# Masked ids mapped by GpSimd ahead of each chunk's gathers, instead of by VectorE once per block

## The chip, the cores and the metric

One core of one Trainium2 chip runs the kernel. The metric is the device time of one execution in microseconds (us); a value is the median of some runs. The program uses the core's five engines: TensorE (PE in the profile, PEld for its weight loads), VectorE (DVE), ScalarE (ACT), GpSimd (POOL) and SyncE (SP). Times are compared within the same rounds on the same chip. Where costs per chunk from different jobs stand side by side, each is taken against the kernel before in its own rounds.

## The reference

A recommendation model: for each of 16384 users, 69 item ids are looked up in a table of 96-wide float32 rows, weighted by a small attention network against a label item, pooled and passed through three dense layers. What matters here is the lookup and its mask:

```python
u = emb[batch_user]                        # 16384 x 69 rows of 96 floats
eff = (batch_user < ITEM_NUM)[..., None]   # ITEM_NUM = 100000; id 100000 is masked
pre = jnp.where(eff, u * att, 0.0)         # a masked token adds nothing
```

The kernels get the mask for nothing by appending a zero row (index 100001) to the table and turning id 100000 into 100001: `row = id + (id >= 100000)`. If the gathered row is zero, so is `u * att`.

## The kernel before

The users are handled in 32 blocks of 512. A block has 69 chunks of 512 tokens (64 main, 5 tail), and a chunk is fetched by four gathers of 128 rows each. Two chunks are a pair; there are 1104 pairs and 2208 chunks. The builder accepts one index per partition for an indirect gather, so one gather fetches at most 128 rows.

```python
def map_ids(n, ids):                       # once per block, 21 steps ahead of its use
    rows = ipool.tile([P, NT], I32, tag="rows", name=f"rows{n}")      # 128 x 276
    nc.vector.scalar_tensor_tensor(rows, ids[:, 0:NT], float(ITEM_NUM), ids[:, 0:NT], ALU.is_ge, ALU.add)
    return rows
...
def fetch(i):                              # one pair of chunks
    u = upool.tile([P, 8, E], F32, tag="u", name=f"u{i}")             # 14 buffers
    ...
    for j in range(2):
        n, k = chunk(2 * i + j)
        ...
        for t in range(4):
            gather(u[:, 4 * j + t, :], rows[n][:, 4 * k + t : 4 * k + t + 1])   # GpSimd
            nc.tensor.transpose(ptr[:, t * P : (t + 1) * P], u[:, 4 * j + t, :], ident)
        ...                                # products on VectorE and ScalarE
```

The attention products follow two steps after the gathers, the pooling products eight; the latter free the `u` buffer.

## Time and profile before

| | before |
|---|---|
| timed, median of 3 (lowest to highest) | 11363.58 us (11353.27 to 11365.34) |
| the one profiled execution | 13499.4 us |
| GpSimd / TensorE busy in it | 63% / 75% |
| a gather: reported time; start to start | 0.951 us; 1.251 us |
| mean granted TensorE clock | 0.658 |

The profiled execution is 2136 us longer than the timed ones; the prediction has to decide what to do about that. In it TensorE hardly ever waits for a gather. This is the row of its waits (who waited <- for what: us in all, times, longest):

```profile
PE ptr L308 <- DMA u<-in_emb,rows: 13.2, 11, 2.0
```

### The profile page before, as it was taken

How to read it: one execution, taken by the hardware profiler on the slowest of the kernel's cores; microseconds unless marked ns; L12 is line 12 of the kernel's file. 1: busy time of each engine (PE TensorE's matmuls, PEld its weight loads, DVE VectorE, ACT ScalarE, POOL GpSimd, SP SyncE). 2: the span in 40 equal slices, each digit the busy share in tenths (PEclk: the TensorE clock that was granted, in tenths of full speed). 3: DMA queues.
4: the chain of work that ended last, by engine and by line, in shares of the span. 5: the costliest groups of instructions: out<-in, count | busy, mean ns of one | idle time of the engine just before them, and what ended most of it. 6: DMA issues, size and time to landing. Idle time of an engine off the chain costs nothing.

```text
span 13499.4 us, 108113 instructions
## 1 busy us (share of the span) xinstructions
PE 10109.4 (75%) x41348; PEld 5068.4 (38%) x41348; DVE 3172.4 (24%) x5424; ACT 3740.6 (28%) x6086; POOL 8525.6 (63%) x8966
## 2 busy tenths in 40 slices
PE   4777777778777776777777777777778777787778
PEld 2333333334333333333333333333333333343334
DVE  2222222222222222222222222222222222222222
ACT  1222222223222222222222222222222222232222
POOL 6666666666666666666666666666666666666664
PEclk5666666666666677666666666766666666666657
DMA  1111111111111111111111111111111111111111
GB/s 37 34 34 35 33 34 33 34 35 34 34 34 34 34 34 33 33 34 34 33 34 34 34 34 35 34 33 33 33 35 34 34 33 34 35 34 33 34 32 22
DMA packets 295008, 453.59 MB, mean 34 GB/s; under 512 B 145952, under 2 KB 151104, under 8 KB 294496
## 3 DMA queue, kind: packets, MB, share of 16 engines
q0 software_dynamic: 286720, 440.98, 15.5%
q8 instruction: 331, 5.42, 0.2%
q1 hardware_dynamic: 6142, 4.77, 0.1%
q14 instruction: 181, 1.48, 0.0%
q10 hardware_dynamic: 1634, 0.94, 0.0%
HBM read 446.04 MB, written 0.07 MB: 33 GB/s over the span
## 4 chain that ended last, share of the span: by engine, by line
PE 62%; another core or an unknown queue 15%; issue 12%; ACT 5%; DVE 5%; POOL 1%; DMA 0%; DVEq 0%; POOLq 0%; ACTq 0%
PE ph L326 22%; PE acc L376 15%; PE ptr L308 9%; PE p L406 5%; PE prow L337 4%; PE ph L278 4%; DVE y L330 3%; ACT y L329 2%; PE patt L353 2%; ACT y L328 1%; PE pa L346 1%; DVE quT L311 1%; ACT uT L319 1%; POOL u L227 1%
## 5 line engine op out<-in xcount | busy, mean ns | idle before, releaser
L227 POOL DMA_INDIRECT u<-in_emb,rows x8832 | 8401.6, 951 | 4802.4 <-issue 2351.7
L376 PEld LDWEIGHTS acc<-rw,u 128*96 128x96 f32 x16384 | 2185.5, 230 | 2828.8 <-issue 2828.2
L278 PE MATMUL ph<-zrow 1*128 1x512 bf16 x1104 | 532.2, 482 | 2654.8 <-DVE y L330 1760.5
L319 ACT COPY uT<-ptr 96x512 f32<-96x512 f32 x2208 | 1285.2, 582 | 3713.4 <-DVE quT L311 2616.7
L376 PE MATMUL acc<-rw,u 128*96 128x20 f32 x16384 | 2298.9, 292 | 1.8 <-DVE rw L359 1.3
L308 PEld LDWEIGHTS ptr<-ident,u 128*96 128x96 f32 x8832 | 1312.6, 167 | 1912.8 <-issue 1547.8
L308 PE MATMUL ptr<-ident,u 128*96 128x128 f32 x8832 | 1785.7, 362 | 326.1 <-issue 247.9
L326 PE MATMUL ph<-uT,A 96*64 96x512 f32 x4416 | 1954.0, 955 | 27.4 <-issue 26.7
L326 PE MATMUL ph<-quT,w 96*64 96x512 f32 x4416 | 1915.7, 909 | 54.5 <-issue 53.2
L328 ACT ACTIVATE y<-ph 128x512 f32<-128x512 f32 x1104 | 659.4, 597 | 4602.9 <-remote 2107.1
L330 DVE TENSOR_TENSOR y<-ph,y 128x512 f32<-128x512 f32 x1104 | 763.7, 692 | 4689.6 <-ACT y L329 2396.5
L311 DVE TENSOR_TENSOR quT<-ptr,qT 96x512 f32<-96x512 f32 x2048 | 1340.0, 680 | 1866.9 <-remote 887.1
L385 DVE COPY pooled<-acc 96x160 f32<-96x160 f32 x1008 | 430.6, 427 | 2811.6 <-remote 1020.7
L326 PEld LDWEIGHTS ph<-quT,w 96*64 96x64 f32 x4416 | 491.4, 202 | 1279.1 <-issue 1277.6
L329 ACT ACTIVATE y<-y,a1c,na1c 128x512 f32<-128x512 f32 x1104 | 897.4, 813 | 37.2
L281 ACT COPY ph<-cT 128x512 f32<-128x512 f32 x1008 | 591.4, 587 | 281.5 <-remote 75.0
L406 PE MATMUL p<-pooled,wf 96*100 96x512 f32 x1280 | 620.0, 625 | 6.3 <-issue 4.8
L337 PE MATMUL prow<-y,v 128*32 128x512 f32 x2208 | 546.6, 932 | 79.7 <-issue 41.3
L326 PEld LDWEIGHTS ph<-uT,A 96*64 96x64 f32 x4416 | 307.0, 183 | 766.4 <-issue 696.0
L339 ACT COPY row<-prow 128x512 f32<-128x512 f32 x276 | 161.4, 585 | 864.0 <-remote 345.4
L353 PE MATMUL patt<-ident,row 128*128 128x128 f32 x1104 | 267.9, 386 | 113.4 <-DVE pre L347 88.1
L406 PEld LDWEIGHTS p<-pooled,wf 96*100 96x100 f32 x1280 | 219.7, 181 | 270.1 <-issue 267.3
(71 smaller groups left out, 2535.6 us busy)
## 6 DMA issues: line engine op xcount, KB each, us to landing
u<-in_emb,rows POOLq DMA_INDIRECT x8832
ids<-in_idx SPq DMA_DIRECT2D x32, 140.0 KB
q<-in_emb,ids POOLq DMA_INDIRECT x128
wf<-in_Wf ACTq DMA_DIRECT2D x1, 825.0 KB
out<-res SPq DMA_DIRECT2D x32, 2.0 KB
w<-in_W SPq DMA_DIRECT2D x1, 96.0 KB
wf<-in_Wf ACTq DMA_DIRECT2D x1, 62.5 KB
a1c<-in_a SPq DMA_DIRECT2D x2, 0.2 KB
```

The costliest lines, as they stand in the source:

```text
L227: nc.gpsimd.indirect_dma_start(out=dst, out_offset=None, in_=emb, in_offset=bass.IndirectOffsetOnAxis(ap=index, axis=0),)
L278: nc.tensor.matmul(ph, zrow[:, 0:P], zrow, start=True, stop=False)
L308: nc.tensor.transpose(ptr[:, t * P : (t + 1) * P], u[:, 4 * j + t, :], ident)
L311: nc.vector.tensor_tensor(quT[:, j, :].rearrange("e (s f) -> e s f", f=FM), ptr.rearrange("e (s f) -> e s f", f=FM), by_field(q[:, k * NS ...
L319: nc.scalar.copy(uT[:, j, :], ptr)
L326: nc.tensor.matmul(ph[j * H1 : (j + 1) * H1, :], w, x[:, j, :], start=False, stop=last)
L328: nc.scalar.activation(y, ph, AF.Sigmoid, scale=S_DICE)
L329: nc.scalar.activation(y, y, AF.Identity, bias=a1c, scale=na1c)
L330: nc.vector.tensor_mul(y, ph, y)
L337: nc.tensor.matmul(pr[32 * k : 32 * (k + 1), :], v2, y, start=True, stop=True)
L376: nc.tensor.matmul(pa[:, j, 2 * t : 2 * t + 2, :].rearrange("e n g -> e (n g)"), u[:, 4 * j + t, :], rw[:, i % 4, j, t, :], start=True, st ...
L406: nc.tensor.matmul(p1, w[:, h * DH : (h + 1) * DH], x, start=(k == 0), stop=(k == KTOP - 1))
```

## The change

The intent is to take the mapping off VectorE and put it on the engine that uses its result, in small pieces that need only small buffers. GpSimd has no fused compare-and-add that compiles (the same `scalar_tensor_tensor` on GpSimd did not compile), so it takes two instructions on a 128x4 tile.

```diff
-    def map_ids(n, ids):
-        rows = ipool.tile([P, NT], I32, tag="rows", name=f"rows{n}")
-        nc.vector.scalar_tensor_tensor(rows, ids[:, 0:NT], float(ITEM_NUM), ids[:, 0:NT], ALU.is_ge, ALU.add)
+    def map_ids(name, ids, k):
+        rows = ipool.tile([P, 4], I32, tag="rows", bufs=8, name=name)
+        i = ids[:, 4 * k : 4 * k + 4]
+        nc.gpsimd.tensor_scalar(rows, i, float(ITEM_NUM), None, ALU.is_ge)
+        nc.gpsimd.tensor_tensor(rows, rows, i, ALU.add)
         return rows
...
+            rows = map_ids(f"rows{i}_{j}", ids[n], k)
             for t in range(4):
-                gather(u[:, 4 * j + t, :], rows[n][:, 4 * k + t : 4 * k + t + 1])
+                gather(u[:, 4 * j + t, :], rows[:, t : t + 1])
...
-            at(first - 21, lambda n=n: rows.__setitem__(n, map_ids(n, ids[n])))
```

More of the change, by code (lines that the diff above doesn't have):

```diff
@@ L103, in load_ids @@
         return ids
-    def map_ids(n, ids):
-        rows = ipool.tile([P, NT], I32, tag="rows", name=f"rows{n}")
-        nc.vector.scalar_tensor_tensor(rows, ids[:, 0:NT], float(ITEM_NUM), ids[:, 0:NT], ALU.is_ge, ALU.add)
-        return rows
-    ids, rows = {0: load_ids(0)}, {}
-    rows[0] = map_ids(0, ids[0])
+    def map_ids(name, ids, k):
[3 more added lines that the diff above has]
+        nc.gpsimd.tensor_tensor(rows, rows, i, ALU.add)
+        return rows
+    ids = {0: load_ids(0)}
     ident = const.tile([P, P], F32, name="ident")
```

## The prediction

> **What bounds the kernel now.** I read the page first, then GpSimd's instructions in order of time, then who waited for whom, then the table of stretches, and last the trace's events.
>
> The page's head and the two rows that matter:
>
> ```profile
> span 13499.4 us, 108113 instructions
> PE 10109.4 (75%) x41348; PEld 5068.4 (38%) x41348; DVE 3172.4 (24%) x5424; ACT 3740.6 (28%) x6086; POOL 8525.6 (63%) x8966
> PE 62%; another core or an unknown queue 15%; issue 12%; ACT 5%; DVE 5%; POOL 1%; DMA 0%; DVEq 0%; POOLq 0%; ACTq 0%
> L227 POOL DMA_INDIRECT u<-in_emb,rows x8832 | 8401.6, 951 | 4802.4 <-issue 2351.7 <-PE acc L376 860.1 <-remote 755.3
> ```
>
> Taken at its word this says TensorE-bound: PE is busiest and is 62% of the chain. But this one profiled execution took 13499 us and the three timed ones 11363.58 us in the median, 2136 us less, so the profile shows the kernel with something in it that the timed runs do not have. Which engine sets 11364 us has to be worked out.
>
> GpSimd in order of time, where nothing holds it up:
>
> ```profile
> 13354.67 0.95 POOL L227 DMA_INDIRECT u<-in_emb,rows  x1 [0.30 <-issue]
> 13355.92 0.94 POOL L227 DMA_INDIRECT u<-in_emb,rows  x1 [0.30 <-issue]
> ...
> 13368.43 0.94 POOL L227 DMA_INDIRECT u<-in_emb,rows  x1 [0.30 <-issue]
> ```
>
> These are 12 gathers; 13368.43 - 13354.67 = 13.76 us over 11 steps is 1.251 us from start to start: 0.95 us of work and 0.30 us in which GpSimd waits for nothing that the profile shows, but cannot start the next. So the 63% of the page understates GpSimd: while it gathers it is full. There are 8832 + 128 = 8960 gathers (the 128 fetch the label rows), and 8960 x 1.251 = 11209 us. The first starts at 3.3 us; the last starts at 13368.4 us and the span ends at 13499.4 us, so some 130 us of draining follow. 3 + 11209 + 130 = 11342 us, 22 us (0.2%) below the timed median. The timed kernel therefore looks bound by the issue of gathers, from end to end.
>
> Why the profiled execution is longer:
>
> ```profile
> POOL u L227 <- issue: 2351.7, 7703, 0.6
> POOL u L227 <- PE acc L376: 860.1, 160, 39.9
> POOL u L227 <- remote: 755.3, 239, 6.0
> POOL u L227 <- PE ptr L308: 447.0, 177, 4.7
> ```
>
> The first row is the 0.30 us between gathers (2351.7 / 7703 = 0.305). The others, with the smaller rows of this view, are 4802.4 - 2351.7 = 2451 us in which GpSimd waited, nearly all for a `u` buffer that TensorE had not yet freed. In the same trace I added up the stretches over 3 us without any TensorE record: 313 of them, 2210 us. An example is 3007 to 3028 us, in which DVE and ACT also stand still and GpSimd goes on until its buffers are full:
>
> ```profile
> 3020.86 0.94 POOL L227 DMA_INDIRECT u<-in_emb,rows  x1 [0.30 <-issue]
> 3027.59 0.95 POOL L227 DMA_INDIRECT u<-in_emb,rows  x1 [5.79 <-remote]
> ```
>
> The chain books such stretches as "another core or an unknown queue" (15% of 13499 us = 2025 us). 2210 us of TensorE silence, 2025 us of unknown chain, and an excess of 2136 us over the timed runs are about the same amount; I read the stalls as belonging to the profiled execution. Without them, a pair of chunks costs TensorE 9.1 us (median over the 492 pairs whose TensorE gaps all stay below 1 us) and GpSimd 8 x 1.251 = 10.0 us. GpSimd is slower by a tenth.
>
> **What the Trainium skill says.** GPSIMD Engine Reference, section 2.1 Instruction dispatch: an instruction is broadcast and dispatched in software on eight cores and counts as complete when all eight have read and their writes have landed in SBUF; consecutive GpSimd instructions are no barrier between cores, so dependent ones need a semaphore wait. The trace agrees in the one place that has such a pair, the building of the identity:
>
> ```profile
> 0.74 0.20 POOL masks.py:197 MEMSET ident<- 128x128 f32 x1 [0.29 <-POOLq L547]
> 1.02 0.29 POOL masks.py:199 TENSOR_SCALAR_AFFINE_SELECT ident<-ident 128x128 f32<-128x128 f32 x1
> ```
>
> The second waits for the first's semaphore in the built program of the kernel before, and starts 0.08 us after its end. Perfetto Trace Analysis, section GPSIMD Engine Instruction, says to time GpSimd from start to start and not by reported durations; that is why I use 1.251 and not 0.951 us. SBUF — State Buffer, section Who interferes with whom: a VectorE instruction with two SBUF inputs blocks GpSimd instructions that read SBUF. The trace before has no steady GpSimd reads, so it can't say; the candidates are the `rw` products (276 of 826 ns) and the last layers' products, together under 3% of the time. GPSIMD Engine Reference, section 4.1 Engine selection, sends elementwise work to VectorE; the present mapping there costs 32 x 432 ns = 14 us on an engine 24% busy.
>
> **The change part by part.**
> Removed: the 32 VectorE instructions, 14 us off the bound. Worth nothing. The first block's mapping ran before the first gathers and delays none (first gather 3.3 us, first `u` gather 8.6 us).
> Added: per chunk of four gathers two GpSimd instructions on 128x4 int32, 2208 chunks, 4416 instructions. They stand in GpSimd's own stream immediately before the gathers that read them, so nothing hides them: GpSimd is strictly in order and full. For one chunk, from the end of its predecessor's last gather:
> - gap to the compare: 0.30 us, taken as that between gathers;
> - compare: 0.12 us (a guess between the one-column memsets, 0.10 to 0.12 us, and the 128-column select, 0.29 us);
> - gap to the add, with its wait for the compare: 0.07 us, from the identity pair;
> - add, two inputs: 0.14 us, likewise;
> - wait of the first gather for the add, up to its start: 0.20 us, the median from a TensorE event to the start of the gather that it released (424 cases, 0.26 us at most).
> Sum 0.83 us, in place of the 0.30 us gap that was there: 0.53 us more per chunk. 2208 x 0.53 = 1170 us, all on the path: 11364 + 1170 = 12534 us, which I round to 12530.
> Also added: reuse of `rows` after eight chunks must wait for the four gathers that read it. Eight chunks are 32 gathers, 40 us, and I expect the waits met long before; extra semaphore instructions (up to a few per chunk) are run ahead by the sequencer while a gather still works. I count 0 for them.
> Moved: GpSimd's cost per pair rises from 10.0 to about 11.1 us, so TensorE gets more idle time. Its granted clock (0.658 mean) may drop, without effect, as it would still need less than GpSimd.
>
> **Rivals.**
> (1) TensorE bounds the timed runs too, and GpSimd has slack. For it: the chain as printed, and 100% - 15% = 85% of 13499 = 11474 us, also near 11364. Against it: the 11342 us floor of GpSimd leaves 22 us of slack, and 4416 instructions at even 0.10 us are 442 us. In this case the time is still 11342 + 1170 = about 12510 us; it changes the reason, not the outcome.
> (2) The small instructions are nearly free: the four first memsets start only 0.03 us apart. They have no waits between them, though; here there are two. If each instruction with its wait cost 0.12 us, it would be 0.24 us a chunk: 11364 + 530 = 11890 us.
> (3) They are dear: the waits empty the queue ahead of GpSimd, so that preparation of the next gather that now lies under the previous one is laid bare, or the VectorE products block the reads. With 0.85 us a chunk: 11364 + 1877 = 13240 us.
> (4) Per-block mapping on VectorE was delaying gathers, and the change frees them. Against: of GpSimd's waits none is for `rows`; the mapping is put 21 steps ahead of its use. No gain.
>
> **Range and chances.** The term that decides is the cost per chunk. I hold 0.27 to 0.79 us likely at 8 in 10: 11364 + 596 = 11960 and 11364 + 1744 = 13108. To stay within 2% (227 us) a chunk would have to cost less than 0.10 us for two instructions and two waits; that needs GpSimd to have hidden slack. 4% for that, 1% for a gain.
>
> **What would show it.** In the changed kernel's trace: 4416 small GpSimd instructions; gathers inside a chunk still 1.251 us apart; the step from the fourth gather of a chunk to the first of the next about 1.78 us where nothing else waits (1.251 + 0.53). GpSimd's waits for TensorE should shrink well below 2451 us, since it is now slower; and the profiled span should grow less than the timed one, to some 13700 to 14400 us, as part of the stalls hides behind the added work. I am wrong if the step at the chunk's border stays near 1.25 us, if gathers within a chunk slow down, or if the timed result moves by something that 2208 steps do not explain.

## The result

| | before | changed |
|---|---|---|
| timed, median of 3 | 11363.58 us | 13387.33 us (13387.23 to 13388.96) |
| profiled execution | 13499.4 us | 13385.5 us |
| GpSimd busy | 63% | 73% |

The ratio is 1.178, 95% interval 1.176 to 1.181. Here and below a ratio is the mean time of one kernel's fast runs over that of the other's of the same rounds, so it is not quite the ratio of the medians. The loss is 13387.33 - 11363.58 = 2024 us, or 2024 / 2208 = 0.917 us a chunk, where 0.53 was predicted. The time lies above the predicted range.

The page of the changed kernel, the lines that answer to those of before (span; engines; chain by engine; groups with busy us, mean ns and idle time ahead of them):

```profile
span 13385.5 us, 113504 instructions
PE 10807.4 (81%) x41348; PEld 5051.0 (38%) x41348; DVE 3213.7 (24%) x5392; ACT 3767.1 (28%) x6086; POOL 9782.8 (73%) x13382
POOL 66%; issue 24%; PE 8%; DMA 2%; POOLq 0%; ACT 0%; DVE 0%; ACTq 0%
...
L228 POOL DMA_INDIRECT u<-in_emb,rows x8832 | 8661.5, 981 | 3243.8 <-issue 2096.8
...
L109 POOL TENSOR_SCALAR rows<-ids 128x4 int32<-128x4 int32 x2208 | 555.2, 251 | 59.5
L110 POOL TENSOR_TENSOR rows<-rows,ids 128x4 int32<-128x4 int32 x2208 | 443.4, 201 | 184.1
```

The chain now runs through GpSimd nearly from end to end (66% work; 24% "issue", mostly its gaps), and there is no "unknown queue" in it. The waits of GpSimd, and the row of TensorE's waits shown above for before:

```profile
POOL u L228 <- issue: 2096.8, 6624, 2.0
POOL u L228 <- POOL rows L110: 1147.0, 2208, 0.8
```

```profile
PE ptr L310 <- DMA u<-in_emb,rows: 2429.5, 2749, 2.7
```

In the steady part GpSimd no longer waits for any other engine. What the profile shows is a wait for itself: 1147.0 us in 2208 waits, 0.52 us each, put down to its own add. (The experiments show that the add is not what ends it.) TensorE waits for gathers instead. One chunk in order of time:

```profile
5000.91 0.94 POOL L228 DMA_INDIRECT u<-in_emb,rows  x1 [0.30 <-issue]
5001.87 0.26 POOL L109 TENSOR_SCALAR rows<-ids 128x4 int32<-128x4 int32 x1
5002.21 0.20 POOL L110 TENSOR_TENSOR rows<-rows,ids 128x4 int32<-128x4 int32 x1
5002.94 1.04 POOL L228 DMA_INDIRECT u<-in_emb,rows  x1 [0.53 <-POOL rows L110]
5004.29 0.95 POOL L228 DMA_INDIRECT u<-in_emb,rows  x1 [0.30 <-issue]
```

From the start of one chunk's first gather to the next chunk's it is 5.884 us in the median, against 5.005 before: 0.879 us more. The parts, means over the 2208 chunks unless noted, beside those of the prediction:

| part | predicted us | measured us | where from |
|---|---|---|---|
| gap to the compare | 0.30 | 0.03 | 59.5 / 2208 |
| compare | 0.12 | 0.25 | group of line 109 |
| gap to the add | 0.07 | 0.08 | 184.1 / 2208 |
| add | 0.14 | 0.20 | group of line 110 |
| add to the start of the first gather | 0.20 | 0.52 | 1147.0 / 2208 |
| the usual gap, replaced | -0.30 | -0.30 | 2351.7 / 7703, before |
| first gather longer than others | 0 | 0.10 | means 1.054 and 0.956 |
| sum | 0.53 | 0.88 | |

0.88 x 2208 = 1943 us; some 81 us of the 2024 are left. The trace has 81 gaps of 0.4 to 2.0 us before a second or fourth gather, 77 us of excess; the undisturbed profile of the kernel before (below) has none. Their cause is open. GpSimd's stream is 4416 arithmetic instructions longer, and one instruction queue has 224 packets where it had 181. But the run below that puts the add before the third gather has as many GpSimd instructions, 225 such packets and not one of these gaps.

### The profile page after: what moved, and what is told of

Same layout as the page of the kernel before. It is cut to its first block, busy times and chain, and to the rows that moved or that the text cites. A ratio compares the mean times of both kernels' runs of the same rounds, so it can differ in the third digit from the quotient of the medians.

```text
span 13385.5 us, 113504 instructions
## 1 busy us (share of the span) xinstructions
PE 10807.4 (81%) x41348; PEld 5051.0 (38%) x41348; DVE 3213.7 (24%) x5392; ACT 3767.1 (28%) x6086; POOL 9782.8 (73%) x13382
## 4 chain that ended last, share of the span: by engine, by line
POOL 66%; issue 24%; PE 8%; DMA 2%; POOLq 0%; ACT 0%; DVE 0%; ACTq 0%
POOL u L228 59%; POOL rows L109 4%; POOL rows L110 3%; PE ph L328 2%; PE p L408 2%; DMA u<-in_emb,rows 2%; PE acc L378 2%; POOL q L228 1%; PE ptr L310 1%; PE prow L339 1%; POOLq L228 0%; PE pa L348 0%; PE ph L279 0%; PE patt L355 0%; ACT y L331 0%
## 5 line engine op out<-in xcount | busy, mean ns | idle before, releaser
L228 POOL DMA_INDIRECT u<-in_emb,rows x8832 | 8661.5, 981 | 3243.8 <-issue 2096.8
L310 PE MATMUL ptr<-ident,u 128*96 128x128 f32 x8832 | 2422.6, 372 | 2498.3 <-DMA u<-in_emb,rows 2429.5
L310 PEld LDWEIGHTS ptr<-ident,u 128*96 128x96 f32 x8832 | 1237.5, 155 | 4833.3 <-DMA u<-in_emb,rows 2916.5
L378 PE MATMUL acc<-rw,u 128*96 128x20 f32 x16384 | 2348.6, 295 | 1.8 <-DVE rw L361 1.3
L328 PE MATMUL ph<-quT,w 96*64 96x512 f32 x4416 | 1758.2, 889 | 0.0
L408 PE MATMUL p<-pooled,wf 96*100 96x512 f32 x1280 | 798.9, 778 | 1.2 <-DVE x L412 0.8
L109 POOL TENSOR_SCALAR rows<-ids 128x4 int32<-128x4 int32 x2208 | 555.2, 251 | 59.5
L110 POOL TENSOR_TENSOR rows<-rows,ids 128x4 int32<-128x4 int32 x2208 | 443.4, 201 | 184.1
L339 PE MATMUL prow<-y,v 128*32 128x512 f32 x2208 | 474.2, 945 | 0.0
L408 PEld LDWEIGHTS p<-pooled,wf 96*100 96x100 f32 x1280 | 273.2, 223 | 358.7 <-issue 356.5
```

Of the source, the lines that this page charges most:

```text
L109: nc.gpsimd.tensor_scalar(rows, i, float(ITEM_NUM), None, ALU.is_ge)
L110: nc.gpsimd.tensor_tensor(rows, rows, i, ALU.add)
L228: nc.gpsimd.indirect_dma_start(out=dst, out_offset=None, in_=emb, in_offset=bass.IndirectOffsetOnAxis(ap=index, axis=0),)
L328: nc.tensor.matmul(ph[j * H1 : (j + 1) * H1, :], w, x[:, j, :], start=False, stop=last)
L378: nc.tensor.matmul(pa[:, j, 2 * t : 2 * t + 2, :].rearrange("e n g -> e (n g)"), u[:, 4 * j + t, :], rw[:, i % 4, j, t, :], start=True, st ...
L408: nc.tensor.matmul(p1, w[:, h * DH : (h + 1) * DH], x, start=(k == 0), stop=(k == KTOP - 1))
```

## The experiments

**Is GpSimd the bound of the kernel before?** One gather of four left out; the fourth transpose and pooling product read the third slice. This is wrong (the comparison with the reference doesn't notice this error).

```diff
-                gather(u[:, 4 * j + t, :], rows[n][:, 4 * k + t : 4 * k + t + 1])
-                nc.tensor.transpose(ptr[:, t * P : (t + 1) * P], u[:, 4 * j + t, :], ident)
+                if t < 3:
+                    gather(u[:, 4 * j + t, :], rows[n][:, 4 * k + t : 4 * k + t + 1])
+                nc.tensor.transpose(ptr[:, t * P : (t + 1) * P], u[:, 4 * j + min(t, 2), :], ident)
...                                       # the pooling product likewise
```

> The kernel before with three gathers per chunk instead of four; the fourth transpose and the fourth pooling product read the third slice (wrong result on purpose, all other work the same). Theory (the timed kernel before is bound by GpSimd's issue of gathers): GpSimd needs only 6752 x 1.2515 + 77 = 8530 us, so TensorE takes over at about 9.1 us a pair of chunks, 10000 to 10500 us. Rival (TensorE bounds the timed kernel before too): no change, 11250 us or more.

It took 9164.99 us against 11343.25 (ratio 0.808). So the timed kernel before was bound by its gathers, by a wide margin: TensorE needs at most 9165 / 1104 = 8.3 us a pair, less than the 9.1 us read from the stalled profile; its mean clock was 0.778 here and 0.658 there.

**Do the stalls belong to profiling?** The kernel before, unchanged, with a new profile.

> The kernel before once more, with another profile. Theory (the stalls of TensorE over 3 us, 2210 us in the profile of before, belong to the profiled execution of this kernel): timed 11364 within 0.3%, and a profiled span again far above it, 12500 us or more. Rival (that profile was a single bad execution): a span within 1% of the timed 11364.

Timed 11341.7 us, and the profiled span was the same: the theory fell, the rival was right. Its span, its chain and the row of TensorE's waits:

```profile
span 11342.1 us, 108113 instructions
POOL 37%; PE 32%; issue 17%; DMA 11%; ACT 2%; DVE 1%; POOLq 0%; ACTq 0%
```

```profile
PE ptr L308 <- DMA u<-in_emb,rows: 1317.0, 1642, 2.2
```

This is what the kernel before looks like when nothing disturbs it: TensorE waits 1317 us for gathers, not 13, and no "unknown queue" is in the chain. It has one TensorE gap over 3 us; the first profile had 313, 2210 us in all. More on the stalls below.

**One instruction per chunk in place of two.** The host writes the zero row at index 100000 itself (no label in the inputs has that id), so that a plain copy of the ids gives the right output.

```diff
-        nc.gpsimd.tensor_scalar(rows, i, float(ITEM_NUM), None, ALU.is_ge)
-        nc.gpsimd.tensor_tensor(rows, rows, i, ALU.add)
+        nc.gpsimd.tensor_scalar(rows, i, 0.0, None, ALU.max)
...                                       # on the host: the zero row
```

> The changed kernel with one GpSimd instruction per chunk in place of two: the compare and the add are replaced by one tensor_scalar (max with 0, which copies the ids), and the host puts the zero row at the masked id itself, so the output stays right. Theory (the cost is a sum of parts laid bare on GpSimd: compare 0.25 + gap 0.08 + add 0.20 + wait to the first gather 0.52 + longer first gather 0.10 + 0.03 - the usual 0.30 gap = 0.88 us a chunk, timed 0.917): only the add and its gap go, 0.28 us, so 13387 - 2208 x 0.28 = about 12770 us. Rival A (the two waits on GpSimd's own semaphore are the cost, half of it each): 12375 us. Rival B (a fixed cost of breaking the stream of gathers once per chunk, however many instructions): at least 13250 us.

It took 12013.4 us against 11343.25 (ratio 1.059), 670 / 2208 = 0.304 us a chunk. All three expectations were too high. Removing the add saved 0.61 us a chunk (0.917 - 0.304), and the add with its gap accounts for 0.28 of that. The rest is in the step to the gather:

```profile
5001.40 0.23 POOL L109 TENSOR_SCALAR rows<-ids 128x4 int32<-128x4 int32 x1
5001.90 1.03 POOL L227 DMA_INDIRECT u<-in_emb,rows  x1 [0.27 <-POOL rows L109]
```

The gather waits for the instruction ahead of it as in the changed kernel, but for 0.27 us, not 0.52. So that wait alone is not what costs 0.52 us.

**The mapping one chunk ahead.** Compare and add of chunk c+1, then the gathers of chunk c.

```diff
-            rows = map_ids(f"rows{i}_{j}", ids[n], k)
+            rows = ahead.pop() if ahead else map_ids(f"rows{i}_{j}", ids[n], k)
+            if 2 * i + j + 1 < 2 * NPAIR:
+                n2, k2 = chunk(2 * i + j + 1)
+                ahead.append(map_ids(f"rowsn{i}_{j}", ids[n2], k2))
```

> The changed kernel with the two GpSimd instructions of a chunk issued one chunk earlier: compare and add of chunk c+1, then the gathers of chunk c. Same instructions, same count; the first gather's wait for the add that feeds it is long over. The add still waits for its compare. Theory (0.52 us from the end of the add to the first gather is mostly the wait's round trip, and an ordinary gap of 0.30 us remains): 0.2 us a chunk saved, 13387 - 2208 x 0.2 = about 12945 us. Rival C (the 0.52 us and the longer first gather are the price of going from arithmetic to a gather, wait or no wait): at least 13250 us.

It took 12896.81 us against 11342.83 (ratio 1.137): close to the theory's 12945, for another reason. The saving falls on every second chunk alone. Two neighbouring chunks:

```profile
5003.63 0.20 POOL L110 TENSOR_TENSOR rowsn<-rowsn,ids 128x4 int32<-128x4 int32 x1
5004.33 1.04 POOL L228 DMA_INDIRECT u<-in_emb,rowsn  x1 [0.51 <-issue]
...
5009.47 0.20 POOL L110 TENSOR_TENSOR rowsn<-rowsn,ids 128x4 int32<-128x4 int32 x1
5009.81 1.04 POOL L228 DMA_INDIRECT u<-in_emb,rowsn  x1
```

0.506 us and 0.146 us (medians; neither varies by more than 3 ns between the 5th and the 95th percentile). The built program shows the difference. In both the add waits for its compare. In the first chunk of a pair the gather has two waits, for an older gather and for TensorE (a new `u` buffer). In the built program only separate semaphore-wait instructions carry two waits and all others at most one, so the other wait goes into such an instruction between add and gather. In the second chunk there is one wait and no such instruction. The Trainium skill, Perfetto Trace Analysis, section Identifying Dependency Chains, says that such instructions "may" be inserted; it gives them no price, and their record lasts 17 ns.

**Compare before the first gather, add before the third.** Both of chunk c+1, among the gathers of chunk c; no instruction waits for the one next to it.

```diff
...
+                nc.gpsimd.tensor_scalar(rows2, ids2, float(ITEM_NUM), None, ALU.is_ge)   # before the four gathers
...
             for t in range(4):
+                if nxt and t == 2:
+                    nc.gpsimd.tensor_tensor(rows2, rows2, ids2, ALU.add)
```

> As the run that maps one chunk ahead, but the compare stands before the chunk's first gather and the add before its third, so that no GpSimd instruction waits for the one just before it. Theory (waits gone, instructions stay): compare 0.25 + add 0.20, each with about 0.03 us ahead of it, 0.51 us a chunk: 11364 + 1130 = about 12490 us. Rival C (each step from arithmetic to gather costs about 0.2 + 0.1 us beyond the usual gap, and there are now two of them): 11364 + 2208 x (0.51 + 0.6) = about 13800 us, slower than the change itself.

It took 12061.55 us against 11342.83 (ratio 1.063), 0.325 us a chunk, less than the theory and far from the rival. The same two instructions cost a third of the 0.917 us. The gaps after them are 0.17 and 0.15 us in place of the usual 0.30, which the theory had not taken off twice. The separate semaphore-wait instruction stands behind the compare here too, in nearly every chunk; as the compare itself isn't held by a wait, it does no harm.

**A third instruction, read by nobody.** One more compare behind the add.

```diff
         nc.gpsimd.tensor_tensor(rows, rows, i, ALU.add)
+        idle = ipool.tile([P, 4], I32, tag="idle", bufs=8, name=name + "x")
+        nc.gpsimd.tensor_scalar(idle, i, float(ITEM_NUM), None, ALU.is_ge)
```

> The changed kernel with one more GpSimd compare per chunk, into a tile that nobody reads, behind the add (no wait on it, so it fills the time in which the first gather waits for the add, or else adds to it). Theory (the first gather's wait is dead time in which GpSimd could work): the 0.25 us compare fits into the 0.52 us, so the time rises by under 0.1 us a chunk, to 13400 to 13600 us. Rival D (every instruction adds its length, the 0.52 us begin after the last of them): 13387 + 2208 x 0.28 = about 14005 us.

It took 13341.14 us against 11342.83 (ratio 1.176, interval 1.174 to 1.178; the change had 1.178, 1.176 to 1.181). The third instruction is free:

```profile
5004.77 0.20 POOL L110 TENSOR_TENSOR rows<-rows,ids 128x4 int32<-128x4 int32 x1
5004.93 0.22 POOL L112 TENSOR_SCALAR rows_0x<-ids 128x4 int32<-128x4 int32 x1
5005.51 1.05 POOL L230 DMA_INDIRECT u<-in_emb,rows  x1 [0.36 <-issue]
```

From the add's end (5004.97) to the gather it is 0.54 us, about as without the extra instruction (medians 0.51 and 0.53 us, in both). That time has room for 0.22 us of work, so in the changed kernel it is not arithmetic that fills it.

**Add first, then the next chunk's compare, then the gathers.** This keeps both instructions side by side, and the gather's wait for an add just issued; only the add's wait for its own compare is over long before.

```diff
-            rows = map_ids(f"rows{i}_{j}", ids[n], k)
+            rows = add(c)              # tensor_tensor on the tile that compare(c) began
+            if c + 1 < 2 * NPAIR:
+                compare(c + 1)         # tensor_scalar into the next tile
...                                       # both are new functions, left out here
```

> The changed kernel with the same two instructions per chunk side by side, in the other order: the add of chunk c, then the compare of chunk c+1, then the gathers of chunk c. The first gather still waits for the add just ahead of it; only the add's wait for its own compare is now over long before. Theory E (what costs is an instruction held by a wait with a separate semaphore-wait instruction behind it: the sequencer cannot run ahead; 0.36 us, seen in the run that maps one chunk ahead, where the step after the add is 0.506 us with such an instruction behind it and 0.146 us without): nothing is held any more except the gather itself, so per chunk add 0.20 + compare 0.25 + two small gaps 0.06 + 0.17 - 0.30 + longer first gather 0.09 = 0.47 us: 11343 + 1030 = about 12370 us, 12200 to 12450. Rival F (the gather's wait for the add next to it is the 0.52 us): 12900 us or more.

```profile
5005.07 0.20 POOL L310 TENSOR_TENSOR rows<-rows,ids 128x4 int32<-128x4 int32 x1
5005.23 0.24 POOL L305 TENSOR_SCALAR rows<-ids 128x4 int32<-128x4 int32 x1
5005.64 1.04 POOL L228 DMA_INDIRECT u<-in_emb,rows  x1 [0.17 <-issue]
```

In the trace the 0.52 us are gone: it is 0.17 us to the gather (0.36 us from the add's end), and 5.406 us from chunk to chunk (0.41 above before). The time could not confirm it. It was 13537.02 us, but on a chip on which the kernel before took 13405.02. The kernel was sent three times more for that reason:

> The run with add of chunk c, compare of chunk c+1, then the gathers, once more and unchanged, because its first time fell on a chip on which TensorE stood still for 2934 us in stretches over 3 us and the kernel before itself took 13405 us. Theory E on a chip without such stretches: the step from chunk to chunk is 5.41 us in its trace against 5.00 of before, so 11343 + 2208 x 0.41 = 12250 us, with the contention seen elsewhere up to 12400, 1.075 to 1.095 times the kernel before. Rival F: 12900 us or more. If this chip stalls as well (before over 12500 us), the time tells nothing and only the steps count.

> The same split order (add of chunk c, compare of chunk c+1, gathers of chunk c), unchanged, sent once more in the hope of a chip on which the kernel before takes 11343 us: theory E 1.075 to 1.095 times the kernel before (about 12200 to 12400 us), rival F 12900 us or more. On a chip where the kernel before takes 13400 us it tells nothing new.

> The split order once more, last try for a chip on which the kernel before takes 11343 us: theory E 1.075 to 1.095 times the kernel before, rival F 1.137 or more. On a stalling chip it tells nothing new.

They took 13522.12, 13677.53 and 13689.75 us against 13409.75, 13578.89 and 13532.35 of before; all fell on stalling chips and tell nothing of the time. The steps were 5.419, 5.407 and 5.407 us.

**Two buffers for `rows`.** This moves the wait for older gathers ahead of the compare, so that the second chunk of each pair has no separate semaphore-wait instruction behind its add.

```diff
-        rows = ipool.tile([P, 4], I32, tag="rows", bufs=8, name=name)
+        rows = ipool.tile([P, 4], I32, tag="rows", bufs=2, name=name)
```

> The changed kernel with two buffers for rows instead of eight. In the built program this moves the wait for the landing of older gathers from ahead of the first gather to ahead of the compare; in every second chunk no separate semaphore-wait instruction is left between add and first gather, in the other one is (for TensorE). Theory E: the step from add to first gather stays at 0.50 to 0.53 us in the first chunk of a pair and falls to about 0.27 us (as in the run with one instruction) in the second: 1104 x 0.24 = 260 us saved against the change, about 13090 us beside 11343 of before. Rival F: both stay at 0.5 us, 13300 us or more. Rival G (fewer buffers make the compare wait for landings): slower than the change, 13450 us or more.

The changed kernel ran in the same rounds:

> The changed kernel itself once more, on the chip and in the rounds of the two others, so that they can be compared with it: 1.178 times the kernel before, 13350 to 13390 us.

It took 13062.46 us, the changed kernel 13361.42: 299 us less, where 260 were expected. Both run at an undisturbed pace on this chip (12 TensorE gaps over 3 us with 60 us in the one, one gap in the other), so these two can be compared; the 13405.02 us of before hold stalls, so a ratio to them (0.974 for two buffers) tells nothing of the cost per chunk. A first and a second chunk:

```profile
5002.65 0.20 POOL L110 TENSOR_TENSOR rows<-rows,ids 128x4 int32<-128x4 int32 x1
5003.35 1.04 POOL L228 DMA_INDIRECT u<-in_emb,rows  x1 [0.51 <-issue]
...
5008.50 0.20 POOL L110 TENSOR_TENSOR rows<-rows,ids 128x4 int32<-128x4 int32 x1
5008.97 1.04 POOL L228 DMA_INDIRECT u<-in_emb,rows  x1 [0.27 <-issue]
```

Put together, the step from the last arithmetic to the first gather (medians):

| add held by a wait for its compare | wait instruction between | gather waits for the arithmetic | step us | run |
|---|---|---|---|---|
| yes | yes | yes | 0.505 to 0.531 | the change |
| yes | yes | no | 0.506 | one chunk ahead, first chunks |
| yes | no | yes | 0.274 | two buffers, second chunks |
| yes | no | no | 0.146 | one chunk ahead, second chunks |
| no (there is no add) | yes | yes | 0.272 | one instruction |
| no | yes | over by then | 0.17 | compare before first, add before third; add first |
| no | no | no | 0.15 | compare before first, add before third: ahead of the third gather |

By itself the held add costs nothing (0.146 us beside 0.15) and the wait instruction some 0.02 us (0.17). Both together cost 0.23 to 0.26 us where the gather waits for the add anyway, and 0.36 us where it doesn't.

The traces' records of the wait instructions show where this comes from; their semaphore numbers tell which gather each belongs to. In the changed kernel the last one before a chunk's first gather is that gather's own, in 2207 of the 2208 chunks, and the gather starts 0.728 us after its end (median; 0.727 to 0.729 us from the 5th to the 95th percentile). The median is the same with the third instruction and in the first chunks of one chunk ahead and of two buffers, whether the gather waits for the add or not. With one instruction per chunk it is already the next chunk's in 2123 chunks: the gather's own had passed some 5.5 us, about a chunk, earlier. And in the first run of the split order, where stalls of TensorE held a gather's own wait instruction (477 times), the gather again started 0.729 us after it (median). So in these runs GpSimd's sequencer passes such instructions a chunk ahead unless something holds it, and the held add takes that lead away. The gather's wait for the add is not what ends last in the changed kernel, although its page says so. A second profile of the same kernel, with nearly the same steps (5.871 us), puts far less down to the add:

```profile
POOL u L228 <- POOL rows L110: 339.3, 653, 0.8
```

What the 0.728 us are spent on, the records do not show. In the changed kernel the wait instruction's record itself lies just ahead of the add's start and lasts 17 to 43 ns.

**The mapping on GpSimd, once per block.**

```diff
-        nc.vector.scalar_tensor_tensor(rows, ids[:, 0:NT], float(ITEM_NUM), ids[:, 0:NT], ALU.is_ge, ALU.add)
+        nc.gpsimd.tensor_scalar(rows, ids[:, 0:NT], float(ITEM_NUM), None, ALU.is_ge)
+        nc.gpsimd.tensor_tensor(rows, rows, ids[:, 0:NT], ALU.add)
```

> The kernel before with the mapping once per block as before, but on GpSimd (two instructions on 128x276, 32 blocks). Theory: 64 instructions of about 0.3 to 0.8 us each on GpSimd's path, no gather waits just behind them, about 1.5 us a block: 11364 + 50 = about 11410 us (within 1%). Rival (arithmetic on GpSimd disturbs its gathers in general): over 11590 us.

It took 11448.2 us against 11343.25 (ratio 1.009), 105 us. The instructions take 0.946 and 0.775 us, 55 us in 32 blocks. The profiles, from two chips, differ by 117 us (11458.7 and 11342.1); the other 62 us fit gathers of 0.951 us in this run and 0.944 in the undisturbed run of before (medians; 7 ns x 8832), which was not followed up. Arithmetic on GpSimd 32 times is no trouble; doing it 2208 times with waits is.

**The mapping by chunks, on VectorE.**

```diff
-        nc.gpsimd.tensor_scalar(rows, i, float(ITEM_NUM), None, ALU.is_ge)
-        nc.gpsimd.tensor_tensor(rows, rows, i, ALU.add)
+        nc.vector.scalar_tensor_tensor(rows, i, float(ITEM_NUM), i, ALU.is_ge, ALU.add)
```

> The changed kernel with the mapping still chunk by chunk, but as one VectorE instruction on the same 128x4 tile (2208 VectorE instructions). Theory: VectorE has room (24% busy), GpSimd carries only gathers, so the time goes back to within 0.5% of the kernel before, 11310 to 11420 us; the mapping must run ahead because VectorE is not in GpSimd's order. Rival (cutting the mapping into 4-column pieces, with eight small buffers and a wait for each, is itself what costs): 12000 us or more.

It took 28572.87 us against 11343.25 (ratio 2.519). The theory was far off. The time lies in the rival's "12000 us or more", but not for the rival's reason:

```profile
5007.73 0.69 DVE L331 TENSOR_TENSOR y<-ph,y 128x512 f32<-128x512 f32 x1 [3.59 <-ACT y L330]
5008.34 0.15 DVE L109 SCALAR_TENSOR_TENSOR rows<-ids 128x4 int32<-128x4 int32 x1
5009.25 0.95 POOL L227 DMA_INDIRECT u<-in_emb,rows  x1 [12.37 <-issue]
```

Of GpSimd's waits, this row names the mapping:

```profile
POOL u L227 <- DVE rows L109: 3550.4, 1118, 12.7
```

In the trace VectorE takes its instructions in program order, and the mapping of a chunk stands behind the products of chunks before it, which wait for their gathers, transposes and products. GpSimd stood idle for 12.37 us until a 0.15 us instruction had its turn. The run-ahead of six pairs (14 `u` buffers less the eight steps to the pooling) is lost. To be sure that the small pieces themselves are free, the same with each piece mapped 32 chunks earlier, in 40 buffers:

```diff
-            rows = map_ids(f"rows{i}_{j}", ids[n], k)
+            while len(ahead) <= AHEAD and mapped[0] < 2 * NPAIR:      # AHEAD = 32
+                n2, k2 = chunk(mapped[0])
+                ahead.append(map_ids(f"rows{mapped[0]}", ids[n2], k2))
+                mapped[0] += 1
+            rows = ahead.pop(0)
...                                       # and bufs=40; the instruction on VectorE as above
```

> As the run with the mapping chunk by chunk on VectorE, 2.5 times as slow as before, but each 128x4 piece is mapped 32 chunks (some 160 us) before its gathers, in 40 buffers. Theory H (that run was slow because VectorE's order put each mapping behind the products of the chunk before, so that gathers could not run ahead; the small pieces themselves are free): within 1% of the kernel before. Rival (2208 small pieces with their waits cost by themselves): 3% or more slower.

> The mapping on VectorE by 128x4 pieces, 32 chunks ahead, unchanged, once more for the same reason. Theory H: within 1% of the kernel before, 11300 to 11450 us on a chip without stalls; rival: 11680 us or more.

It took 13404.57 us against 13409.75 (ratio 0.999), and 13649.93 against 13578.89 (1.005). Both chips stalled, so the times would hide a small cost on GpSimd, but the cost of 2.5 times is gone, and in the trace gathers follow each other every 1.25 us across chunk borders (median 1.249 us, chunk to chunk 4.996 us):

```profile
5002.97 0.94 POOL L227 DMA_INDIRECT u<-in_emb,rows  x1 [0.30 <-issue]
5004.22 0.94 POOL L227 DMA_INDIRECT u<-in_emb,rows  x1 [0.30 <-issue]
```

So the small pieces are not the cause. This run changed the order and the number of buffers together; that it was the order is read from the lines above, where GpSimd had issued every earlier gather over 12 us before, so that no buffer of `rows` was missing, and the mapping started right behind VectorE's product.

**The stalls.** The jobs on chips 1 and 6 had the kernel before at 11343 us, those on chips 5 (twice), 2 and 8 at 13405, 13410, 13579 and 13532 us. In the traces from the latter, kernels with chunk steps of 5.0 to 5.4 us show 306 to 344 TensorE gaps over 3 us, 2187 to 2962 us in all. On chip 5 the changed kernel, with steps of 5.9 us, shows one, and with two buffers, 5.8 us, 12. There the change costs nothing: 13361.42 against 13405.02 us, ratio 0.996. And two buffers are faster than the kernel before: 13062.46 us, ratio 0.974 (0.972 to 0.976). The slower pace of gathers goes with fewer stalls; why is not shown. TensorE's load alone doesn't bring the stalls about: with a gather left out it was 93% busy on chip 1 without any. Of the jobs of the experiments those with stalls all came later than those without, so chip and hour can't be told apart there; the first profile, which stalled too, came before all of them, and its chip isn't recorded. The cause is open.

On the chips without stalls no run with a right result beats the kernel before: every variant with arithmetic on GpSimd that ran there costs more, and VectorE's mapping was never on the path. What would help there is fewer or shorter gathers, as leaving out one in four shows. A gather with four indices per partition did not build.

## Why the prediction was wrong

**The bound: right.** GpSimd's issue of gathers sets the time of the kernel before. Leaving out a quarter of them gives 9165 us, and the undisturbed profile has GpSimd waiting for nearly nothing and TensorE for gathers. The floor of 11342 us met the span of that profile, 11342.1 us, more closely than its rounding deserves.

**"I read the stalls as belonging to the profiled execution": wrong.** They were absent from the timed runs, so the number was not hurt, but profiling does not bring them: later profiles have none, and on other chips the runs of before took 13400 us or more. With this falls the forecast of a profiled span of 13700 to 14400 us: it was 13385.5 us, the timed value. One reading was off on the way: the 2451 us hold the ordinary gap of 0.305 us of 1129 gathers too, some 340 us. GpSimd's real waits were some 2110 us.

**Position of the cost: right.** All of it lies on GpSimd's path, 2208 times, and on a chip without stalls nothing hides it.

**The size per chunk: wrong, and this is why the time fell outside the range.** The failing step is "wait of the first gather for the add, up to its start: 0.20 us", together with "extra semaphore instructions ... are run ahead by the sequencer while a gather still works. I count 0 for them". The step measured 0.52 us. The 0.20 us came from gathers released by TensorE. In the built program these have a wait instruction ahead of them too, but no held arithmetic ahead of that. The experiments with one chunk ahead, two buffers and one instruction show that the semaphore instruction is not free behind an add that is itself held by a wait: without it the step is 0.27 us. That, 0.25 us a chunk, makes 550 us; without it the sum would be 0.63 us, inside the range of 0.27 to 0.79. The wait instruction is run ahead, as the prediction had it, only where nothing ahead of it is held; behind the held add it was not, and the gather started 0.728 us after it. Even without that the sum would have been above the forecast: the compare and the add took 0.45 us and not the guessed 0.26, and the first gather after arithmetic took 0.10 us longer, which no one had asked about. The gap to the compare, 0.03 us and not 0.30, went the other way.

**The rivals.** The first fell with the gather left out, and the fourth with the result: no gain came. The third named 13240 us and came nearest. Its first half, "the waits empty the queue ahead of GpSimd" and lay the next gather's preparation bare, is close to what the records show: the held add takes the sequencer's lead away and lays 0.728 us bare, and the spread order pays 0.325 us for the same two instructions. That this time is the gather's preparation is not shown. Rival 2's 0.24 us a chunk lies below those 0.325 us, and no order reached it. The third's other half, VectorE's products, is no part of the difference. Long gathers do go with them: 143 of the 157 gathers over 1.2 us in the changed kernel overlap the `rw` product with its two SBUF inputs, but only 197 of the other 8675, as the section Who interferes with whom of the Trainium skill's SBUF page would have it for a GpSimd instruction that reads SBUF. But the undisturbed profile of before has nearly as many (147 long gathers, 101 of them over that product).

**What would show it.** The step across the border of a chunk was to be 1.78 us; its median is 2.03. GpSimd's waits for TensorE were to shrink well below 2451 us; the profile of the changed kernel has none. Gathers within a chunk were to stay 1.251 us apart; the second and third steps did (1.255), the first is 1.35.

## What to carry to other kernels

On the engine that sets the time, price a small instruction by the steps it puts between its neighbours, with its waits and where the program puts the other waits of the next instruction, not by its own length: here two instructions of 0.45 us in all cost 0.92 us when each waited for the one just ahead, and 0.33 us when none did. Before moving work to an in-order engine, ask what stands ahead of it there: on VectorE the same mapping leaves the gathers' pace as it was when issued far ahead, and costs 17000 us just in time. And when a profiled execution and the timed ones differ by a fifth, profile again before reading waits from it.

## What the Trainium skill lacked or had wrong

- GPSIMD Engine Reference, section 2.1, asks for a wait where a GpSimd instruction reads what another of its cores wrote just before, but has no price for a wait between two GpSimd instructions: 0.08 us from a compare to the add that waits for it, 0.27 us to a gather, 0.51 to 0.53 us to a gather when a held add and a separate semaphore-wait instruction come together.
- Perfetto Trace Analysis, section Identifying Dependency Chains, tells of the inserted semaphore instructions without a cost; behind a held instruction one costs 0.23 to 0.36 us, though its record has 17 to 43 ns; the gather behind it starts 0.73 us after it where it was not passed ahead.
- GPSIMD Engine Reference, section 4.1, calls one-input work on GpSimd "roughly line-rate" and two-input work slower. Here the one-input int32 compare on 128x276 took 0.946 us and the two-input add 0.775 us (1.01 and 0.93 us from start to the next start); on 128x4 they took 0.25 and 0.20 us. VectorE's one instruction for both took 0.43 us on 128x276; the compare alone was not run there.
- No page has the issue cost of an indirect gather: 0.95 us for 128 rows, 1.25 us from start to start, and 0.08 to 0.11 us more for the first gather after the mapping.
- No page tells of TensorE stalls as on chips 2, 5 and 8: some 2200 to 3000 us of 13500 in gaps over 3 us.
